# A two-layer graph network on one core: edge sums in units of two chunks, and transfers in prime numbers of rows

## The chip, the cores and the metric

The kernel runs on one core of a Trainium2 chip. The metric is device time in microseconds (us) from launch to end; lower is better. The engines are named as in the profile: PE (TensorE, matrix products), PEld (PE's loading of the stationary operand), DVE (VectorE), ACT (ScalarE), POOL (GpSimd) and SP (SyncE, which only issues transfers). Each engine executes its own instructions in the order in which they are written, and waits on semaphores for the others.

## The reference, cut to what matters

N = 6250 nodes carry 160 numbers each: 64 scalars and 32 vectors of three. E = 200000 edges run from a node `src` to a node `dst`; they are sorted by `dst`. Each edge has four attributes (`sh` in the kernel, `edge_attr_4`) and ten features (`ea`, `edge_attr_10`). There are two layers, each a sum over edges followed by small products and a normalization.

```python
# layer 0: m is bilinear in x[src] and the edge's four attributes
m_agg = segment_sum(m, dst, N)                 # (N, 160)
x = layernorm(x + (x + relu(linear(m_agg))))
# layer 1: l0, l1 = two linear maps of x times node_vec1
h = relu(edge_attr_10 @ W_fc1 / sqrt(10)) * sqrt(2)     # (E, 100)
w = h @ W_fc2 / sqrt(100)                               # (E, 192): w0 64, w1 64, w2 32, w3 32
y0, y1 = l0[src], l1[src]
m0 = w0*y0*e0;  m1 = (w1*y0) x e1;  m2 = w2*e0*y1;  m3 = w3*dot(y1, e1)
out = layernorm(x + linear(x) + linear(segment_sums of m0..m3))
```

All is float32. Because layer 0's message is linear in x[src] and in each attribute, the kernel first sums, for each destination node and each of the four attributes, attribute times x[src], and applies the weights once per node afterwards.

## The kernel before

**Chunks and windows.** The edges are padded to 391 chunks (`NCH`) of 512: 128 partitions times `J` = 4 edges. Since `dst` is sorted, the edges of one chunk end in a narrow window of at most 32 nodes (`W`; `WIDTHS` sets 16, 24 or 32 by the chunk's number, and 32 for the first three). From chunk 312 (`HALF`) on, a chunk has two windows, one for each half of the partitions. `ORDER` interleaves the chunks below `HALF` with those above; `POS` gives a chunk's place in it, and `CLOSE` the step by which a block of 128 nodes has all its edges. There are 49 blocks (`NB`). `windowed` is the path that is executed; it calls `sums(0, x)` and `sums(1, ytab)`, where `ytab` is the table of node values that layer 0 writes to DRAM.

**One chunk in layer 0.** `load` has GpSimd issue four indirect transfers (`gathered`, L206), each fetching 128 rows of x by `srcs` into one of eight buffers `g`, and now and then has SP load edge attributes (`attributes`: up to 32 chunks as four transfers of up to 32 rows into `raw`, which `turn` transposes on DVE). `onehot` builds the chunk's stationary operand on DVE: L381 compares the relative destinations with 0, 1, ... into `bank`, a PSUM tile, and L385 multiplies that by the attributes into `S`, one of three slots of `ring` (128 partitions x 4 edges x 4 attributes x 32 places, of which the first 16, 24 or 32 are written). `matmuls` adds four products on PE (L427), each S(128 x 128) transposed times g(128 x 160), into a PSUM tile `ab`; each product waits for its own gather. A chunk above `HALF` has eight products of 64 rows. `add` transposes `ab` in blocks of 32 x 32 (L447) and adds it to `acc` at the window's place (L449), both on DVE.

**One chunk in layer 1.** The sources are rows of `ytab`. `features` of four chunks are loaded by `load` as two transfers of 10 rows from `ea` (into `et` or `early`). `hidden` multiplies them by `W_fc1` for two chunks at a time (PE, `ph`, L394) and has ACT apply relu (`h`, L397). `message` works in halves of two edges per partition: two products `pw` (L407) into one of two PSUM buffers, then three DVE instructions that multiply `pw` by the gathered rows into `m` (L410, and L415 twice). `matmuls` (L427, now 320 columns) and `add` (L444, L445, L449) follow.

**Order.** `sums` writes the order by hand. In step t, each stage treats the chunk that is a fixed number of steps back, and all engines' instructions are written in this order:

```python
stages = [(load, 0), (onehot, 1), (hidden, 1), (add, 4), (message, 2), (matmuls, 3)]   # layer 1
stages = [(load, 0), (onehot, 1), (add, 3), (matmuls, 2)]                              # layer 0
```

After the stages of a step come the `parts`, which finish a block of nodes whose step has come: in layer 0 `fetch` (xt), `project` (ph, L461), `rectify` (rl, L497, and the clearing of acc, L498, on ACT), `residual` and `moments` (L471, L473), `deviation`, `normed` (L478, L480), `turned` (xp, L511, L512), `kept`, `linear` (pl, L525, L526) and `written`, which sends y to `ytab` from ACT and base to `btab` from SP; in layer 1 `fetch_base`, `project_last` (L548), `residual_last`, `deviation` and `sent`. Small weights are prepared at step 8. The four gathers of the first two chunks are issued before the window table is ready, into `early`.

So PE's order in layer 0 is: the four products of a chunk, then whatever part of a block is due. A gather may be issued when the chunk that had the same buffer eight chunks earlier has been multiplied.

## Time and profile before

The times of three runs are 4875.3, 4870.28 and 4859.52 us (median 4870.28). The profiled execution is one more.

| | |
|---|---|
| profiled execution, its own time | 4865.16 us |
| its span, first to last instruction | 4863.0 us |
| instructions | 42324 |
| mean granted clock of PE in the span | 0.752 of full speed |
| busy: PE / PEld / DVE / ACT / POOL | 2968.4 / 2222.4 / 2162.4 / 377.9 / 2973.9 us |
| gathers of x (layer 0) / of ytab (layer 1) | 1556 / 1564, 949 ns each on POOL |
| products of layer 0 (L427, g) | 3744, 716.6 us busy |
| products of layer 1 (L427, m) | 3760, 1087.9 us busy |
| pw (L407) | 3128, 737.3 us busy |
| transposes of layer 0 (L447) | 470, 361 ns each |
| messages (L410 / L415) | 782 of 420 ns / 1564 of 346 ns |
| S (L385) / one-hot (L381) | 782 of 552 ns / 782 of 256 ns |

PE shows each product as two records. How to read the views: in the table of waits a row gives the engine and line, what released it, the total, the number and the longest. In the timeline a row gives start and duration in us, engine, line, operation, output and inputs, shape, how many equal instructions follow one another, and in brackets the idle time before it and its releaser. A releaser called "remote" is a semaphore event next to which no instruction's end was recorded; "issue" is time in which the engine waited for nothing that the profile shows. The ends of PE's instructions are modelled.

### The profile page before, as it was taken

To read this page: it belongs to the slowest core of one execution; us is meant where nothing else is said; L and a number is where in the kernel's file an instruction comes from. 1 tells how busy PE (TensorE), PEld (TensorE's weight loads), DVE (VectorE), ACT (ScalarE), POOL (GpSimd) and SP (SyncE) were. 2 spreads that over 40 slices of the span, in tenths; PEclk is the share of its full clock that TensorE was granted. 3 is DMA by queue.
4 is the path that set the end of the run, shared out by engine and by line. 5 is a ranking of instruction groups with operands and counts; after the bars stand their busy time and mean duration, and the time that the engine had idled before them with its cause. 6 is when DMAs were issued, how large, how long until landed. Compare 5 with 4: busy or idle time off the path is not lost.

```text
span 4863.0 us, 42324 instructions
## 1 busy us (share of the span) xinstructions
PE 2968.4 (61%) x12714; PEld 2222.4 (46%) x12715; DVE 2162.4 (44%) x6948; ACT 377.9 (8%) x747; POOL 2973.9 (61%) x3137
## 2 busy tenths in 40 slices
PE   2333344444444444446587878777878788887777
PEld 1322333333333333434355555555555555555555
DVE  3222222232323333334355555555566566666656
ACT  2000000000000000001000000000100010101000
POOL 5666666666666666664665655565556656555553
PEclk7566655666666666667788888888888888888888
DMA  2222222222222222222222222222222222222221
GB/s 67 61 62 58 63 64 63 61 65 65 66 63 69 64 67 65 69 68 57 57 59 54 60 54 60 57 61 58 59 59 57 62 60 62 61 57 61 58 59 39
DMA packets 198246, 295.60 MB, mean 61 GB/s; under 512 B 59271, under 2 KB 140669, under 8 KB 198011
## 3 DMA queue, kind: packets, MB, share of 16 engines
q0 software_dynamic: 150144, 256.45, 21.4%
q1 hardware_dynamic: 40702, 31.55, 2.3%
q10 hardware_dynamic: 7164, 4.80, 0.3%
q8 instruction: 107, 1.75, 0.1%
q14 instruction: 129, 1.05, 0.1%
HBM read 280.57 MB, written 12.00 MB: 60 GB/s over the span
## 4 chain that ended last, share of the span: by engine, by line
PE 42%; another core or an unknown queue 33%; DVE 12%; issue 10%; POOL 2%; ACT 1%; DMA 0%; DVEq 0%; ACTq 0%; POOLq 0%
PE ab L427 24%; PE pw L407 11%; PE ph L394 3%; DVE m L415 3%; DVE S L385 2%; PE ph L461 2%; POOL g L206 2%; DVE acc L449 1%; PE bank L548 1%; DVE m L410 1%; DVE ab L444 1%; DVE ab L447 1%; DVE ab L445 1%; DVE bank L381 1%
## 5 line engine op out<-in xcount | busy, mean ns | idle before, releaser
L206 POOL DMA_INDIRECT g<-ytab,srcs x1564 | 1484.3, 949 | 1074.1 <-issue 438.5
L206 POOL DMA_INDIRECT g<-in_x,srcs x1556 | 1477.2, 949 | 741.8 <-issue 424.3
L427 PE MATMUL ab<-g,S 128*128 128x160 f32 (+1 forms) x3744 | 716.6, 392 | 818.6 <-issue 418.0
L427 PE MATMUL ab<-m,S 128*128 128x320 f32 (+1 forms) x3760 | 1087.9, 493 | 56.1 <-DVE acc L449 48.0
L427 PEld LDWEIGHTS ab<-g,S 128*128 128x128 f32 (+1 forms) x3744 | 638.5, 259 | 902.5 <-issue 441.2
L407 PE MATMUL pw<-fc,h 100*128 100x192 f32 x3128 | 737.3, 385 | 472.4 <-DVE m L415 375.1
L407 PEld LDWEIGHTS pw<-fc,h 100*128 100x128 f32 x3128 | 609.3, 222 | 703.1 <-issue 313.2
L427 PEld LDWEIGHTS ab<-m,S 128*128 128x128 f32 (+1 forms) x3760 | 698.3, 220 | 324.3 <-issue 161.9
L447 DVE STREAM_TRANSPOSE ab<-ab 128x160 f32<-128x160 f32 x470 | 169.6, 361 | 1232.0 <-remote 999.1
L385 DVE TENSOR_TENSOR S<-bank,sh 128x384 f32<-128x384 f32 (+2 forms) x782 | 431.5, 552 | 551.8 <-remote 189.8
L415 DVE TENSOR_TENSOR m<-g,pw 128x192 f32<-128x192 f32 x1564 | 475.9, 346 | 0.0
L410 DVE TENSOR_TENSOR m<-pw,g 128x256 f32<-128x256 f32 x782 | 328.1, 420 | 320.0 <-remote 208.9
L397 ACT ACTIVATE h<-ph 100x512 f32<-100x512 f32 x391 | 230.6, 597 | 2223.2 <-remote 983.1
L449 DVE TENSOR_TENSOR acc<-acc,ab 128x120 f32 (+2 forms) x940 | 261.7, 278 | 285.1 <-remote 176.3
L381 DVE TENSOR_TENSOR bank<-iota,rel 128x96 f32<-128x96 f32 (+2 forms) x782 | 200.2, 256 | 181.9 <-remote 96.9
L461 PE MATMUL ph<-wb,acc 128*128 128x160 f32 (+1 forms) x490 | 125.4, 430 | 246.9 <-DVE acc L449 107.2
L461 PEld LDWEIGHTS ph<-wb,acc 128*128 128x128 f32 (+1 forms) x490 | 109.6, 286 | 264.3 <-issue 117.1
L445 DVE STREAM_TRANSPOSE ab<-ab 32x160 f32<-32x160 f32 x470 | 165.5, 352 | 16.2
L444 DVE STREAM_TRANSPOSE ab<-ab 128x160 f32<-128x160 f32 x470 | 167.4, 356 | 10.7 <-issue 6.7
L394 PE MATMUL ph<-early,fc 10*100 10x512 f32 x392 | 114.9, 648 | 0.3
L394 PE MATMUL ph<-et,fc 10*100 10x512 f32 x390 | 112.0, 642 | 0.2 <-issue 0.2
L525 PE MATMUL pl<-wn,xT 128*128 128x320 f32 (+1 forms) x98 | 49.4, 593 | 87.1 <-issue 60.2
(80 smaller groups left out, 732.3 us busy)
## 6 DMA issues: line engine op xcount, KB each, us to landing
g<-ytab,srcs POOLq DMA_INDIRECT x1564
g<-in_x,srcs POOLq DMA_INDIRECT x1556
raw<-in_sh SPq DMA_DIRECT2D x88, 64.0 KB
early<-in_ea SPq DMA_DIRECT2D x98, 40.0 KB
xt<-in_x SPq DMA_DIRECT2D x48, 80.0 KB
ytab<-y ACTq DMA_DIRECT2D x48, 80.0 KB
btab<-base SPq DMA_DIRECT2D x48, 80.0 KB
et<-in_ea SPq DMA_DIRECT2D x96, 40.0 KB
```

The costliest lines, as they stand in the source:

```text
L206: nc.gpsimd.indirect_dma_start(out=g[:, j, :], out_offset=None, in_=table, in_offset=bass.IndirectOffsetOnAxis(ap=srcs[:, c, j:j + 1], axi ...
L381: nc.vector.tensor_tensor(oh[:, :, :w], iota[:, None, :w].to_broadcast([P, J, w]), rel[:, c, :, None].to_broadcast([P, J, w]), op=ALU.is_e ...
L385: nc.vector.tensor_tensor(S[c][:, :, :, :w], oh[:, :, None, :w].to_broadcast([P, J, 4, w]), attr[:, :, :, None].to_broadcast([P, J, 4, w]) ...
L394: nc.tensor.matmul(ph[:, i, :], fc1[g:g + 10, :], ET[c // 4][g:g + 10, c % 4 // 2, :], start=True, stop=True)
L397: nc.scalar.activation(H[c], H["p"][:, c % 2, :].rearrange("f (p j) -> f j p", j=J), AF.Relu, scale=FC_SCALE)
L407: nc.tensor.matmul(pw[:, j, :], h[:, q + j, :], fc2, start=True, stop=True)
L410: nc.vector.tensor_tensor(mq[:, :, :, 0:64], pw[:, :, 0:128].rearrange("p j (a u) -> p j a u", a=2), y[:, :, None, 0:64].to_broadcast([P, ...
L415: nc.vector.tensor_tensor(mq[:, :, a, 64:160].rearrange("p j (d u) -> p j d u", d=3), y1, pw[:, :, None, w:w + 32].to_broadcast([P, 2, 3, ...
L427: nc.tensor.matmul(ab[:, :n], one[h * i:h * i + h, j, :, :], t[h * i:h * i + h, j, :], start=(j == 0), stop=(j == J - 1), skip_group_check ...
L447: nc.vector.transpose(tr, blocks[:, 0])
L449: nc.vector.tensor_tensor(v, v, tr[:, :, :width(c)], op=ALU.add)
L461: nc.tensor.matmul(po[:r], lhs, weights[:, g, :], start=(g == 0), stop=(g == 4))
```

## The change

**Pairs.** The gather buffers become four pairs, `g` of 2 x 4 x 160, and the ring of S two pair slots. `onehot` works at every second step on two chunks: one comparison (L401), one multiplication (L408); `turn` writes the attributes in another order so that a pair's lie side by side. `WIDTHS` puts the first four chunks at width 32 where it were three. In layer 1 `onehot` stands one step later.

**Layer 0's sums.** For two chunks below `HALF`, `matmuls` issues one product of eight columns (one from each of the pair's gather buffers) into a spare part of the PSUM tile (L461), and then the eight products (L467). A chunk above `HALF` is a unit by itself, with four columns. In the built program all the waits for gathers then stand ahead of L461, and the products after it carry none. `add` transposes the pair with one instruction (L480); the additions stay one per window (L496). There are two PSUM tiles of two banks where there were four of one.

**Layer 1's messages.** The four `pw` products of a chunk (L430) go to one tile of two banks, of which there is one, and three DVE instructions (L433, and L438 twice) make the chunk's messages.

**Transfers.** The features are first copied, in eight parts during layer 0, from `ea` to a DRAM table `etab` of 17 rows (ten, and seven of them again), and layer 1 loads 17 rows from it, three steps earlier than before and ahead of the gathers' step (`features`). Edge attributes are loaded as groups of 30 chunks in transfers of 31 rows (or 17, 19, 23 or 29), one transfer per step over four steps, and `raw` is always cleared first. Blocks of 128 rows (xt, base, ytab, btab, out) are sent as 94 and 34 rows.

**In the built programs** SP's issues rise from 530 to 738 and ACT's from 49 to 95; GpSimd's gathers stay as they are. PE's stand-alone waits go from 476 to 1010 in layer 0 and from 944 to 551 in layer 1; PE's instructions that post to its semaphore go from 1687 to 439 and from 1881 to 1562. DVE's element-wise instructions go from 1256 to 864 and from 3594 to 2033.

```diff
-WIDTHS = ((3, 32), (128, 16), (208, 24), (HALF, 32), (NCH, 24))
+WIDTHS = ((4, 32), (128, 16), (208, 24), (HALF, 32), (NCH, 24))
...
+LEADS = 94
+ROWS = 17
+STEP = 30
+COPIES = 8
+LEAD = 3
...
+def group(c):
+    begin, end = (0, HALF) if c < HALF else (HALF, NCH)
+    first = c - (c - begin) % STEP
+    return first, 31 if end - first >= STEP else next(n for n in (17, 19, 23, 29, 31) if n >= end - first)
...
-    ring = const.tile([P, 3, J, 4, W], F32, name="S")
+    ring = const.tile([P, 2, 2, J, 4, W], F32, name="S")
...
-            pa = s.enter_context(tc.tile_pool(name=f"pa{layer}", bufs=3 if layer else 4, space=PSUM))
+            pa = s.enter_context(tc.tile_pool(name=f"pa{layer}", bufs=3 if layer else 2, space=PSUM))
...
-                pp = s.enter_context(tc.tile_pool(name="pp", bufs=2, space=PSUM))
+                pp = s.enter_context(tc.tile_pool(name="pp", bufs=1, space=PSUM))
...
             def load(c):
+                i, half = divmod(POS[c], 2)
+                if not half:
+                    GP[i] = early if not layer and c in ahead else gp.tile([P, 2, J, D], F32, name="g")
+                G[c] = GP[i][:, half]
                 if layer or c not in ahead:
+                    gathered(nc, G[c], srcs, table, c)
+                for first, n in GROUPS:
+                    for q in range(4):
+                        if POS[c] == fetched[first] + (q if POS[first] >= fetched[first] + 4 else 0):
+                            attributes(first, n, q)
...
             def onehot(c):
+                if POS[c] % 2:
+                    return
+                n = min(2, NCH - c)
...
+                oh = bank[:, :n * J * W].rearrange("p (j n) -> p j n", n=W)
+                nc.vector.tensor_tensor(oh[:, :, :w], iota[:, None, :w].to_broadcast([P, n * J, w]),
+                                        rel[:, c:c + n, :].rearrange("p c j -> p (c j)")[:, :, None].to_broadcast([P, n * J, w]),
+                                        op=ALU.is_equal)
+                pair = ring[:, POS[c] // 2 % 2]
...
             def message(c):
...
-                for q in range(0, J, 2):
-                    pw = pp.tile([P, 2, 192], F32, name="pw")
...
+                pw = pp.tile([P, J, 256], F32, name="pw")
+                for j in range(J):
+                    nc.tensor.matmul(pw[:, j, 0:192], h[:, j, :], fc2, start=True, stop=True)
...
+            def unit(c):
+                if layer or c >= HALF:
+                    return [c]
+                return [c - 1, c] if POS[c] % 2 else []

             def matmuls(c):
...
+                    both = PA["unit", c] = pa.tile([P, 2, 512], F32, name="ab")
+                    PA[c] = [both[:, i, :n + D] for i in range(2)]
+                    rows = GP[POS[c] // 2][:, :, :, 0:1] if len(chunks) > 1 else G[c][:, None, :, 0:1]
+                    nc.tensor.matmul(both[:, 0, n + D:n + D + J * len(chunks)], S[chunks[0]][:, 0, :, :],
+                                     rows.rearrange("p a j o -> p (a j o)"), start=True, stop=True, skip_group_check=True)
...
             def add(c):
...
+                    nc.vector.transpose(both[:, :, D:2 * D], both[:, :, 0:D])
...
+            def sent_rows(engine, b, to, from_):
+                cut = LEADS if CLOSE[b] < NCH - 8 and rows(b) == P else rows(b)
+                for part in (slice(0, cut), slice(cut, rows(b))):
+                    if part.start < part.stop:
+                        engine.dma_start(to[part], from_[part])
...
-                stages = [(load, 0), (onehot, 1), (hidden, 1), (add, 4), (message, 2), (matmuls, 3)]
+                stages = [(load, 0), (features, -LEAD), (onehot, 2), (hidden, 1), (add, 4), (message, 2), (matmuls, 3)]
...
+                if not layer and t >= 2 * PREPARE and t % 32 == 0 and t // 32 <= COPIES:
+                    part = slice((t // 32 - 1) * (NCH * CH // COPIES), t // 32 * (NCH * CH // COPIES))
+                    nc.sync.dma_start(etab[0:10, part], ea[:, part])
+                    nc.sync.dma_start(etab[10:ROWS, part], ea[0:ROWS - 10, part])
```

## The prediction

> **What bounds the kernel now.** I read the table by stage first, because the page's shares average two unlike layers. I set its four stretches by GpSimd's gathers: first free gather to last of layer 0, the gap between the layers, the gathers of layer 1, the end. The columns are the stretch, its length, and the busy time and instructions of PE, PEld, DVE, ACT and POOL, then the granted clock and the DMA share.
>
> ```profile
> 31.80:2248.40 2216.60, 916.03 (x4378) 775.84 (x4378) 645.25 (x1995) 123.08 (x273) 1476.28 (x1556) 0.63 0.26 65
> 2248.40:2291.80 43.40, 33.24 (x180) 22.15 (x180) 22.60 (x77) 10.97 (x33) 0.96 (x2) 0.80 0.11 32
> 2291.80:4806.80 2515.00, 1973.11 (x7899) 1392.37 (x7900) 1436.16 (x4649) 238.32 (x428) 1483.37 (x1563) 0.85 0.23 59
> 4806.80:4863.00 56.20, 45.97 (x258) 32.06 (x258) 42.96 (x145) 5.54 (x12) 0.95 (x1) 0.99 0.07 18
> ```
>
> No engine is full in either layer. GpSimd comes nearest: each gather is 949 ns busy and is followed by 0.30 us that the waits call issue, so 1.2525 us at best (timeline: 1211.19, 1212.44, 1213.69, 1214.95). A chunk has four, 5.01 us. Layer 0's 1556 steps need 1949 us of 2217, so GpSimd stood still for 268; layer 1's 1564 need 1958 of 2515, so 557. The whole span is then 32 + 1949 + 268 + 43 + 1958 + 557 + 56 = 4863. Without the stalls, 4038 is the floor that this change leaves, as it removes no gather. So the question is who makes GpSimd wait. The first two rows below are waits of layer 0 (100 to 2250 us), the rest of layer 1 (2292 to 4807): engine, line, releaser, total us, times, longest.
>
> ```profile
> DVE ab L447 <- remote: 964.9, 131, 22.4
> ACT rl L497 <- remote: 714.1, 18, 361.7
> ...
> POOL g L206 <- DVE bank L381: 383.6, 103, 8.8
> PE pw L407 <- DVE m L415: 375.1, 100, 29.1
> ...
> DVE m L410 <- remote: 208.9, 76, 11.9
> DVE S L385 <- remote: 189.8, 29, 20.6
> POOL g L206 <- DVE m L415: 172.5, 49, 7.0
> ```
>
> "Remote" is a release near which no instruction ends. With one core there is no other core, and L447 waits for PE alone. The timeline shows what it is (PE's rows, then DVE's, then GpSimd's):
>
> ```profile
> 1184.81 3.63 PE L427 MATMUL ab<-g,S 128*128 128x160 f32 x24
> 1196.40 3.00 PE L461 MATMUL ph<-wb,acc 128*128 128x160 f32 x10 [7.96 <-DVE ab L447]
> 1199.19 3.86 PE L427 MATMUL ab<-g,S 128*128 128x160 f32 x16
> 1217.44 0.47 PE L511 MATMUL xp<-ident,z 128*128 128x128 f32 x1 [14.39 <-DVE rs L478]
> ...
> 1210.96 0.37 DVE L447 STREAM_TRANSPOSE ab<-ab 128x160 f32<-128x160 f32 x1 [13.87 <-remote]
> ...
> 1216.63 0.28 DVE L449 TENSOR_TENSOR acc<-acc,ab 128x120 f32 x1 [5.31 <-remote]
> ...
> 1211.19 0.95 POOL L206 DMA_INDIRECT g<-in_x,srcs  x1 [2.78 <-remote]
> ```
>
> By the program's counts, the transpose at 1210.96 waits for the last of the three chunks in the run of 24, which ended at 1188.4. Its completion was seen 22 us late, and GpSimd's gather, which needs the same buffer back, was freed by it too. PE meanwhile waited for DVE (14.39). So the bound is a ring in which PE, DVE and GpSimd wait for completions of PE that are posted late. PE's semaphore shows how: in such stretches its updates come singly, at 1199.73, 1203.93, 1208.13, 1210.93 and 1216.61; later nine come 0.04 us apart (1218.02 to 1218.36). One update is one instruction that posts, whatever its step.
>
> I counted those instructions in the built programs: 1687 in layer 0 and 1881 in layer 1 before; 2217 / 1687 = 1.31 us and 2515 / 1881 = 1.34 us for each. The likeness suggests that posting is the pace of both layers; it does not prove it.
>
> **The change, part by part.**
>
> *Layer 0's sums by pairs.* Before, every product of a chunk waits for its own gather and posts by itself: eight posts for two chunks. After, all waits stand before one small product, and the eight follow without a wait and post once. Posts fall from 1687 to 439. Here the page "TensorE: Matmul & The Clock Gate", section "The cost: per-tile semaphore tail", speaks against a gain: it prices a serial completion increment at about 26 ns. By that, 1248 fewer posts are 33 us of latency, nearly all under GpSimd's 5.01 us a chunk, and the change gives layer 0 nothing. The bursts (40 ns) fit the rule; the 1.4 to 5.7 us between single posts do not. I take the row: at 1.31 us, 439 posts need 575 us in 1949, and the layer goes at GpSimd's pace. The worst spacing above, 5.7 us, for 439 posts is 2500 us, but that worst case was not met on average even by the old layer. I leave 30 us of stall (bounds 5 and 150), which is 238 us off.
>
> *What it adds there.* 235 waiting products, 8 columns wide; no row shows one. Nearest is xp at 0.35 us, two records each: 235 x 0.7 = 165 us of PE, which is busy 916 of 2217 us; hidden. Without the cover, those 165. A pair's products now start when its eighth gather has landed, 5 us later than the first chunk's did; four pairs of buffers (40 us of gathers) cover that. PE's stand-alone waits rise from 476 to 1010; behind them queue only products that need the same gathers.
>
> *One-hots and S by pairs.* From L381 (96 columns 257 ns, 128 columns 290) and L385 (384: 558, 512: 692) a column costs 1.03 and 1.05 ns. A pair at width 24 is 0.36 + 0.96 = 1.32 us against 2 x 0.815: 0.16 us less per chunk. Layer 0's transposes (160: 361 ns) become one of 320, 0.53 by that slope: 0.10 less. In layer 0 both are hidden by the gathers. What counts in layer 1 is the distance: S has two pair slots, whose last readers ran two steps before, where the old third slot was read in the step just before. The wait of L385 (remote 190, PE ab 150, PE ph 74, over 1.0 us per chunk) goes. It returns in part at the transposes of the sums, which now wait for the same product of the step before.
>
> *Messages in three instructions.* 2 x (420 + 2 x 346) = 2.22 us per chunk become, at 1.16 ns a column (346 to 420 for 64 columns), 0.72 + 2 x 0.57 = 1.86: 0.37 less, 145 us of DVE in the layer. Posts of pw: two to one. Against it: pw has a single buffer, so the next four products wait for all three messages. Their cover on PE is the sums of the chunk before: about 2.1 us at full clock, more otherwise, and half a ph.
>
> *Layer 1's sum.* PE is busy 1973 / 391 = 5.05 us per chunk, and that work stays. Its wait for messages was 375 / 391 = 0.96. Posts fall from 1881 to 1562, so the pace of 1.34 would give 2093 us, 5.35 per chunk. From below GpSimd gives 5.01; from above 6.43 (no gain). I take PE's 5.05 plus 0.4 for what remains of its waits: 5.45, near the count of posts. Stalls: (5.45 - 5.01) x 391 = 172 instead of 557, 385 us off.
>
> *Transfers in odd numbers of rows.* The page "DMA: Bandwidth & Descriptors", section "Why a DMA increments its semaphore by 16 and not by 1", says that the engines used are the largest number up to 16 that divides the slowest dimension: 17 or 31 rows go to one, 94 and 34 to two. That speaks against this part. Queue q1's 40702 packets took 2.3% of 16 engines, 44 ns for 775 B; by size 2 KB is an estimated 116 ns. A feature load (17 rows, 34 packets) is then 3.9 us on one engine. Four chunks have two: 7.9 us in 20, and by the rule a quarter of that engine is gathers'. Full it is not, and loads are issued three steps earlier. I take 0 (bounds -30 to +60; a share of the late posts could be DMA completions' fault). The issues on SP rise from 530 to 738; over 4.8 ms that is one in 6.5 us.
>
> *Copies of the features, eight of 1.7 MB, and DVE's clearing of raw (under 0.5 us, 26 times).* By the same packet rate, a copy is some 4 us on ten engines; a gather may land late, which the eight in flight (10 us) absorb. I take 10 us, bounds 0 and 60.
>
> Sum: 4863 - 238 - 385 + 10 = 4250. The profiled execution took 4865.16 us for its span of 4863.0, and the median of the runs is 4870.28; I add nothing more, 4250.
>
> **The rivals.**
>
> *Only layer 0 gains.* Layer 1's loop of messages keeps 6.43 us because the single pw buffer takes the place of the S wait. For it: PE waits more for messages than anything else. Against it: PE runs the sums just then. 4038 + 30 + 557 + 10 = 4635.
>
> *Late posts are not a matter of their number.* If what delays a post is PE's waiting itself, fewer posts wait longer each, and more stand-alone waits make it no better. Layer 0 keeps its stalls, DVE's shorter work is hidden: 4863 less at most some 100 us of messages, 4760 to 4870.
>
> *The single buffer makes it slower.* At half clock (layer 1 has 0.85 on average) four pw products take 2.6 us, twice the 1.28 of full clock; a late post like those of L410 (208.9 / 76 = 2.75 us) and 1.86 us of messages make 7.2 in series if PE's sums cover nothing. Layer 1 is then 391 x 7.2 = 2815, the total 4038 - 1958 + 2815 + 30 + 10 = 4935. It decides from 7.05 us per chunk on, if layer 0 gains, as that eats 238 + 557.
>
> **How the numbers follow.** Both layers gain: 0.72, by itself 4090 to 4440 (layer 1 at 5.05 to 5.9 us). Only layer 0: 0.16. Not a matter of number: 0.06, a quarter of it within 0.3%. Slower: 0.06. The range must reach to the rival at 4635 to leave out no more than 2 in 10: 4080 to 4640. 0.3% of 4870, 15 us, is about what the measurement can tell from no change. Faster 0.92, same 0.02, slower 0.06.
>
> **What would show it.** Layer 0's gathers at 1.25 us without gaps, in 1.96 to 2.0 ms; L447's successor without remote waits of 10 us and more; DVE's S without a wait on PE in layer 1; gathers there in 2.0 to 2.3 ms; messages at 0.72 and 0.57 us. The prediction is wrong if the remote waits stay as long with a quarter of the posts, if PE's wait for messages grows beyond 1 us per chunk, or if gathers wait for their own landing behind one loaded DMA engine.

## The result

The changed kernel is slower: 5009.94 us median (4986.77 to 5021.54) beside 4872.78 us (4859.52 to 4875.3) for the kernel before, a ratio of 1.0281 with a 95% interval of 1.024 to 1.0323. The forecast was 4250 us, in a range of 4080 to 4640. Its profiled execution took 4986.77 us, with a span of 4985.0 us.

The table by stage of the changed kernel, with edges at its own first and last gathers (stretch, length, busy time and instructions of PE, PEld, DVE, ACT and POOL, granted clock, DMA share, GB/s):

```profile
32.40:2256.60 2224.20, 994.42 (x4848) 847.70 (x4850) 576.87 (x1400) 122.38 (x275) 1474.52 (x1555) 0.65 0.27 71
2256.60:2300.10 43.50, 34.06 (x184) 22.73 (x180) 19.45 (x59) 9.86 (x31) 0.95 (x1) 0.77 0.12 32
2300.10:4936.50 2636.40, 1935.41 (x7938) 1361.37 (x7940) 1354.37 (x3148) 240.65 (x431) 1484.48 (x1564) 0.83 0.23 58
4936.50:4985.00 48.50, 38.91 (x220) 26.89 (x217) 34.54 (x98) 4.05 (x9) 0.91 (x1) 0.96 0.07 19
```

Layer 0 takes 2224 us where it took 2217, although its PE now posts 439 times and not 1687. Layer 1 takes 2636 where it took 2515; that is 121 of the 122 us that the spans differ by. DVE's work in layer 1 fell from 1436 to 1354 us and bought nothing.

The groups of the page that answer to the edits (busy time and mean ns, then idle time before and its main releaser):

```profile
L480 DVE STREAM_TRANSPOSE ab<-ab 128x320 f32<-128x320 f32 x235 | 123.9, 527 | 1417.1 <-remote 1148.6
L433 DVE TENSOR_TENSOR m<-pw,g 128x512 f32<-128x512 f32 x391 | 270.1, 691 | 801.5 <-remote 390.7
L461 PE MATMUL ab<-g,S 128*128 128x8 f32 (+1 forms) x468 | 105.8, 298 | 560.0 <-issue 382.8
L438 DVE TENSOR_TENSOR m<-g,pw 128x384 f32<-128x384 f32 x782 | 394.1, 545 | 0.0
L408 DVE TENSOR_TENSOR S<-bank,sh 128x768 f32<-128x768 f32 (+2 forms) x392 | 370.1, 944 | 13.4
```

The instructions cost what was estimated, and S's idle time went from 551.8 to 13.4 us. But the remote wait of layer 0's transpose, 964.9 us in 131 places before, is 1144.2 us in 99. ("Remote" stands here for completions of PE that are seen late, as the prediction read it.) The table of waits, the first two rows from 100 to 2250 us and the others from 2400 to 4900:

```profile
DVE ab L480 <- remote: 1144.2, 99, 27.4
...
POOL g L219 <- remote: 239.9, 73, 5.7
...
PE pw L430 <- DVE m L438: 441.8, 103, 11.8
...
POOL g L219 <- DVE m L438: 392.9, 72, 12.6
...
DVE m L433 <- remote: 369.7, 60, 8.8
POOL g L219 <- DVE bank L401: 276.7, 52, 9.5
...
DVE m L433 <- DMA g<-ytab,srcs: 119.3, 47, 5.5
```

The last row is new beside the kernel before: messages wait for gathers that have not landed. GpSimd is held for up to 12.6 us, and then PE and DVE overtake it.

The timeline of layer 0 shows a late completion from both sides:

```profile
1335.77 3.25 PE L467 MATMUL ab<-g,S 128*128 128x160 f32 x10
...
1340.69 0.30 PE L467 MATMUL ab<-g,S 128*128 128x160 f32 x1 [1.68 <-issue]
...
1343.36 0.94 POOL L219 DMA_INDIRECT g<-in_x,srcs  x1 [0.30 <-issue]
1343.48 0.42 PE L467 MATMUL ab<-g,S 128*128 128x160 f32 x1 [2.49 <-issue]
1344.88 0.43 PE L467 MATMUL ab<-g,S 128*128 128x160 f32 x1 [0.98 <-issue]
1346.28 0.63 PE L467 MATMUL ab<-g,S 128*128 128x160 f32 x1 [0.97 <-issue]
1347.68 0.42 PE L467 MATMUL ab<-g,S 128*128 128x160 f32 x1 [0.77 <-issue]
1348.38 0.42 PE L467 MATMUL ab<-g,S 128*128 128x160 f32 x1 [0.28 <-issue]
1348.48 0.53 DVE L480 STREAM_TRANSPOSE ab<-ab 128x320 f32<-128x320 f32 x1 [13.62 <-remote]
1348.72 0.95 POOL L219 DMA_INDIRECT g<-in_x,srcs  x1 [4.41 <-remote]
```

These products wait for nothing that the profile shows, and still their starts fall 0.7, 1.4 or 2.8 us apart. The last of them starts 4 us after GpSimd has run out of buffers (its last gather ended at 1344.3); DVE's transpose and GpSimd's next gather follow at once.

### The profile page after: what moved, and what is told of

The parts are those of the page before. It is cut to its first block, busy times and chain, and to the rows that moved or that the text cites. A ratio compares the mean times of both kernels' runs of the same rounds, so it can differ in the third digit from the quotient of the medians.

```text
span 4985.0 us, 40848 instructions
## 1 busy us (share of the span) xinstructions
PE 3002.8 (60%) x13184; PEld 2258.7 (45%) x13185; DVE 2001.0 (40%) x4786; ACT 376.9 (8%) x747; POOL 2973.2 (60%) x3137
## 4 chain that ended last, share of the span: by engine, by line
PE 35%; another core or an unknown queue 23%; issue 15%; POOL 14%; DVE 9%; DMA 3%; DVEq 0%; ACT 0%; POOLq 0%; ACTq 0%
PE ab L467 19%; POOL g L219 14%; PE pw L430 11%; DVE m L438 3%; PE ph L418 3%; DMA g<-ytab,srcs 2%; DVE m L433 2%; DVE S L408 1%; PE ph L515 1%; DMA g<-in_x,srcs 1%; DVE acc L496 1%; PE ab L461 1%; PE bank L602 1%; DVE bank L401 1%
## 5 line engine op out<-in xcount | busy, mean ns | idle before, releaser
L467 PE MATMUL ab<-m,S 128*128 128x320 f32 (+1 forms) x3760 | 1069.4, 491 | 57.9 <-issue 29.4
L430 PE MATMUL pw<-fc,h 100*128 100x192 f32 x3128 | 709.8, 378 | 642.7 <-DVE m L438 475.7
L430 PEld LDWEIGHTS pw<-fc,h 100*128 100x128 f32 x3128 | 593.0, 218 | 869.2 <-issue 768.8
L467 PE MATMUL ab<-g,S 128*128 128x160 f32 (+1 forms) x3744 | 743.1, 396 | 275.3 <-issue 264.3
L467 PEld LDWEIGHTS ab<-m,S 128*128 128x128 f32 (+1 forms) x3760 | 682.6, 219 | 323.9 <-issue 172.0
L467 PEld LDWEIGHTS ab<-g,S 128*128 128x128 f32 (+1 forms) x3744 | 638.9, 261 | 299.3 <-issue 297.5
L480 DVE STREAM_TRANSPOSE ab<-ab 128x320 f32<-128x320 f32 x235 | 123.9, 527 | 1417.1 <-remote 1148.6
L433 DVE TENSOR_TENSOR m<-pw,g 128x512 f32<-128x512 f32 x391 | 270.1, 691 | 801.5 <-remote 390.7
L461 PE MATMUL ab<-g,S 128*128 128x8 f32 (+1 forms) x468 | 105.8, 298 | 560.0 <-issue 382.8
L438 DVE TENSOR_TENSOR m<-g,pw 128x384 f32<-128x384 f32 x782 | 394.1, 545 | 0.0
L461 PEld LDWEIGHTS ab<-g,S 128*128 128x128 f32 x468 | 102.8, 267 | 628.1 <-issue 538.9
L408 DVE TENSOR_TENSOR S<-bank,sh 128x768 f32<-128x768 f32 (+2 forms) x392 | 370.1, 944 | 13.4
L496 DVE TENSOR_TENSOR acc<-acc,ab 128x120 f32 (+2 forms) x940 | 261.8, 278 | 185.6 <-remote 107.5
L493 DVE STREAM_TRANSPOSE ab<-ab 128x160 f32<-128x160 f32 x470 | 168.9, 359 | 329.2 <-remote 124.1
L401 DVE TENSOR_TENSOR bank<-iota,rel 128x192 f32<-128x192 f32 (+2 forms) x392 | 138.9, 354 | 99.1 <-remote 68.8
```

What stands on the lines that cost most here:

```text
L401: nc.vector.tensor_tensor(oh[:, :, :w], iota[:, None, :w].to_broadcast([P, n * J, w]), rel[:, c:c + n, :].rearrange("p c j -> p (c j)")[:, ...
L408: nc.vector.tensor_tensor(pair.rearrange("p c j k n -> p (c j) k n")[:, :n * J, :, :w], oh[:, :, None, :w].to_broadcast([P, n * J, 4, w]), ...
L430: nc.tensor.matmul(pw[:, j, 0:192], h[:, j, :], fc2, start=True, stop=True)
L433: nc.vector.tensor_tensor(mq[:, :, :, 0:64], pw[:, :, 0:128].rearrange("p j (a u) -> p j a u", a=2), y[:, :, None, 0:64].to_broadcast([P, ...
L438: nc.vector.tensor_tensor(mq[:, :, a, 64:160].rearrange("p j (d u) -> p j d u", d=3), y1, pw[:, :, None, w:w + 32].to_broadcast([P, J, 3, ...
L461: nc.tensor.matmul(both[:, 0, n + D:n + D + J * len(chunks)], S[chunks[0]][:, 0, :, :], rows.rearrange("p a j o -> p (a j o)"), start=True ...
```

## The experiments

Edits are told against the kernel that is named. Kernels of one group ran on one chip, with the kernel before among them, and ratios are taken within a group. The first comparison, of before and after, is a group of its own. One thing has to be known: in groups 2 and 3 the kernel before took 3980 and 3982 us, in the others 4928, 4877 and 4875; group 2 and group 5 used the same chip. In groups 2 and 3 no completion was late, and with the edits of the kernel before GpSimd issued without a gap. The kernel with seven buffers in layer 1 shows it; its layer 0 is that of before. Its layer 0 in group 3 (from 32 to 2000 us), and the wait of its transposes from 100 to 1950 us, where the kernel before had waited for "remote":

```profile
32.00:2000.00 1968.00, 1442.31 (x4558) 918.89 (x4558) 680.76 (x2072) 134.25 (x306) 1473.58 (x1556) 0.57 0.27 73
...
DVE ab L447 <- PE ab L427: 1000.6, 357, 4.6
```

The longest wait is 4.6 us and not 22.4, and no wait of that table is put down to "remote". Layer times in the table are from first to last gather of the profiled execution.

| group | kernel | time, us | ratio to before (95%) | layer 0 | layer 1 |
|---|---|---|---|---|---|
| 1 | messages of before | 4994.27 | 1.0146 (1.0101 to 1.0191) | 2234 | 2623 |
| 1 | transfers of before | 5054.77 | 1.0249 (1.0186 to 1.0313) | 2232 | 2707 |
| 1 | one-hots by chunk in layer 1 | 5090.95 | 1.0352 (1.0303 to 1.0402) | 2233 | 2719 |
| 1 | single-chunk gather buffers in layer 1 | 4870.15 | 0.9892 (0.9846 to 0.9938) | 2237 | 2500 |
| 2 | before, seven buffers in layer 1 | 3981.44 | 1.0004 (0.9995 to 1.0012) | 1945 | 1955 |
| 2 | single buffers and messages of before | 4008.31 | 1.0068 (1.0051 to 1.0084) | 1962 | 1963 |
| 2 | more products in layer 0 | 4009.62 | 1.0073 (1.0053 to 1.0093) | 1962 | 1959 |
| 2 | narrow gathers in layer 0 | 3991.63 | 1.0033 (1.0021 to 1.0045) | 1947 | 1957 |
| 3 | the changed kernel again | 4012.17 | 1.0073 (1.0056 to 1.0089) | 1962 | 1959 |
| 3 | before, pairs of buffers in layer 1 | 3983.15 | 1.0001 (0.9993 to 1.001) | 1946 | 1956 |
| 3 | before, seven buffers in layer 1 | 3983.46 | 1.0002 (0.9994 to 1.0011) | 1946 | 1956 |
| 3 | more products in layer 0 | 4010.56 | 1.007 (1.005 to 1.009) | 1964 | 1960 |
| 4 | before, pairs of buffers in layer 1 | 5007.12 | 1.0278 (1.0221 to 1.0335) | 2218 | 2644 |
| 4 | transfers of before | 4972.97 | 1.0187 (1.0142 to 1.0233) | 2219 | 2636 |
| 4 | more products in layer 0 | 4892.58 | one run | 2265 | 2485 |
| 5 | before, seven buffers in layer 1 | 4872.26 | 0.9999 (0.9979 to 1.0019) | 2216 | 2511 |
| 5 | single buffers and transfers of before | 4821.52 | 0.9893 (0.987 to 0.9915) | 2217 | 2483 |
| 5 | narrow gathers in layer 0 | 4832.74 | one run | 2220 | 2479 |

### Four parts of the change, each undone

After the first comparison the theories were: A, the single pw buffer puts late completions and messages in series; B, the pairs of gather buffers shorten GpSimd's lead; C, the transfers load few DMA engines.

Messages of before, in the changed kernel:

```diff
-pp = s.enter_context(tc.tile_pool(name="pp", bufs=1, space=PSUM))
+pp = s.enter_context(tc.tile_pool(name="pp", bufs=2, space=PSUM))
...
-                pw = pp.tile([P, J, 256], F32, name="pw")
+                for q in range(0, J, 2):
+                    pw = pp.tile([P, 2, 192], F32, name="pw")
...
```

> The changed kernel with the messages of before (two halves, six instructions, two pw buffers). Theory A, the single pw buffer puts PE's late completions and the messages in series: layer 1 falls from 2636 us to about 2520 (as before), the total to about 4890. Theory B, pairs of gather buffers: layer 1 stays within 30 us of 2636, since only 145 us of hidden DVE work come back. Theory C, transfers on few DMA engines: stays too. Layer 0 stays at 2224 in all.

Transfers of before, in the changed kernel:

```diff
-STEP = 30
+STEP = 32
...
-    return first, 31 if end - first >= STEP else next(n for n in (17, 19, 23, 29, 31) if n >= end - first)
+    return first, min(STEP, end - first)
...
-                cut = LEADS if CLOSE[b] < NCH - 8 and rows(b) == P else rows(b)
+                cut = rows(b)
...
-                        nc.sync.dma_start(et[64 * i:64 * i + ROWS, :, :], etab[...])
+                        nc.sync.dma_start(et[64 * i:64 * i + 10, :, :], ea[...])
...
-                    nc.sync.dma_start(etab[0:10, part], ea[:, part])
-                    nc.sync.dma_start(etab[10:ROWS, part], ea[0:ROWS - 10, part])
```

> The changed kernel with the transfers of before (no etab, 10, 32 and 128 rows, one transfer each; features still three steps early). Theory C, rows in prime numbers load one or two DMA engines and gathers land late: DVE's 119 us of waits for landed gathers in layer 1 go and the total falls by 60 to 120 us. Theories A and B: within 20 us of the changed kernel.

One-hots by chunk in layer 1:

```diff
-                if POS[c] % 2:
+                if POS[c] % 2 and not layer:
                     return
-                n = min(2, NCH - c)
+                n = 1 if layer else min(2, NCH - c)
...
-                pair = ring[:, POS[c] // 2 % 2]
+                pair = ring[:, POS[c] // 2 % 2, POS[c] % 2:]
```

> The changed kernel with layer 1's one-hots and S built for each chunk by itself (four slots, lag two as in the changed kernel). DVE has 0.16 us more a chunk. If the pair's longer instructions (1.3 us at once) hold up messages, layer 1 falls by 20 to 60 us; by theories A, B and C it moves by less than 20 us.

Gather buffers of one chunk in layer 1:

```diff
                 i, half = divmod(POS[c], 2)
-                if not half:
+                if layer:
+                    G[c] = gp.tile([P, J, D], F32, name="g1")
+                elif not half:
...
+        with tc.tile_pool(name="gl", bufs=GRING) as gp:
+            sums(1, ytab, gp, hp)
```

> The changed kernel with layer 1's gather buffers of one chunk each (eight, as before) in place of four pairs. Theory B, a pair's first gather waits for the messages of the pair's second chunk, so the depth is seven chunks and not eight: layer 1's stalls of 680 us fall by about 100 and the total to about 4900. Theories A and C: within 20 us.

Only the buffers bring back more than the loss: ratio 0.9892, with layer 1 at 2500 us. Theory B is right about the place. With the transfers undone the kernel is still 2.5% slower than before (1.9% in group 4), so C is not the cause of the loss in layer 1. With the messages of before the interval (1.0101 to 1.0191) ends below that of the changed kernel in its own comparison (from 1.024), so beside the pairs the new messages cost about 1.3%. The edit undoes the single pw buffer and the longer instructions together; as the longer ones are less work for DVE, the buffer is the likelier part, but that was not separated. It is not what decides, since the kernel with single gather buffers has these messages too and is faster than before. One-hots by chunk were to gain 20 to 60 us in layer 1 or to change little; they gave 1.0352 and 2719 us there. The intervals overlap, so that a loss is not certain; why there should be one is open.

What the buffers changed in layer 1, from the table of waits from 2400 to 4700 us, the changed kernel first:

```profile
POOL g L219 <- DVE m L438: 327.1, 61, 12.6
POOL g L219 <- DVE bank L401: 273.2, 51, 9.5
DVE m L433 <- DMA g<-ytab,srcs: 100.8, 41, 5.5
```

```profile
POOL g L219 <- DVE m L441: 191.8, 63, 6.6
POOL g L219 <- DVE bank L404: 162.7, 65, 5.1
...
DVE m L436 <- DMA g<-ytab,srcs: 8.3, 9, 1.8
```

GpSimd's longest stops are half as long, and messages hardly ever find gathers missing.

### Pairs of buffers alone, and seven buffers, in the kernel before

Is it the depth that the pairs take away, or the pair itself? Two edits of the kernel before, in layer 1 alone:

```diff
-                if layer or c not in ahead:
-                    G[c] = gathered(nc, gp.tile([P, J, D], F32, name="g"), srcs, table, c)
+                if layer:
+                    i, half = divmod(POS[c], 2)
+                    if not half:
+                        G["pair"] = gp.tile([P, 2, J, D], F32, name="g")
+                    G[c] = gathered(nc, G["pair"][:, half], srcs, table, c)
...
+        with tc.tile_pool(name="gl", bufs=GRING // 2) as gp:
+            sums(1, ytab, gp, hp)
```

```diff
+        with tc.tile_pool(name="gl", bufs=7) as gp:
+            sums(1, ytab, gp, hp)
```

Seven buffers, group 2; then pairs and seven buffers, group 3:

> The kernel before with seven gather buffers in layer 1 in place of eight, nothing else. Theory B, the depth of the gather buffers is what the pairs took away: layer 1 grows by 60 to 190 us, and the total is 1 to 4% above before. If depth is not what counts (only that a pair's eight gathers are released at once), it stays within 0.5% of before.

> The kernel before with one part of the change alone: layer 1's gather buffers are four pairs. Where completions are late, the pairs alone give layer 1 at least the 120 us that the whole change lost there: ratio 1.02 to 1.04. If the pairs cost only together with the single pw buffer, within 0.5% of before. Where gathers run without gaps: within 0.3%.

> The kernel before with seven gather buffers in layer 1. Where completions are late: layer 1 grows by 60 to 190 us if depth is what counts, and by less than 20 us if it is the release of eight gathers at once. Where gathers run without gaps: within 0.3%, as it was there.

In groups 2 and 3 nothing stalls, and both are within 0.1% of before. So the pairs by themselves cost nothing there. Once more where completions are late, the pairs in group 4 and seven buffers in group 5:

> The kernel before with four pairs of gather buffers in layer 1, nothing else. Where completions are late: layer 1 grows by at least 120 us, ratio 1.02 to 1.04, if the pairs by themselves are the cause; within 0.5% of before if they cost only together with the single pw buffer or the longer one-hots. Where completions are in time: within 0.3%, as it was.

> The kernel before with seven gather buffers in layer 1. Where completions are late: if depth counts, layer 1 grows by 60 to 130 us (ratio 1.012 to 1.027); if it is the release of eight gathers at once, by less than 20 us (within 0.4%). Where they are in time: within 0.3%, as it was twice.

The pairs alone give 1.0278, as much as the whole change (1.0281). Seven buffers give 0.9999: depth is not the cause, and theory B's reason falls while its place stands. Each stands beside the kernel before of its own group (4877 and 4875 us). The two programs differ in one thing. A pair's first gather waits for exactly the value of DVE's semaphore that the same gather waits for with seven buffers (all 187 such waits beyond the first 64 gathers are equal); with seven buffers GpSimd waits 192 more times, at the second chunk of each pair. PE's and DVE's posts are the same in number (3567 and 4844). So **192 waits were taken from GpSimd, none was added, and the kernel became 2.8% slower**.

GpSimd's timeline, the last gather of a run and the next, from 3000 to 3060 us; with seven buffers:

```profile
3013.50 0.95 POOL L206 DMA_INDIRECT g<-ytab,srcs  x1 [0.30 <-issue]
3017.60 0.95 POOL L206 DMA_INDIRECT g<-ytab,srcs  x1 [3.16 <-DVE bank L381]
...
3021.62 0.95 POOL L206 DMA_INDIRECT g<-ytab,srcs  x1 [0.30 <-issue]
3024.88 0.94 POOL L206 DMA_INDIRECT g<-ytab,srcs  x1 [2.31 <-DVE bank L381]
...
3038.65 0.94 POOL L206 DMA_INDIRECT g<-ytab,srcs  x1 [0.30 <-issue]
3044.01 0.95 POOL L206 DMA_INDIRECT g<-ytab,srcs  x1 [4.41 <-DVE bank L381]
```

and with pairs:

```profile
3013.80 0.95 POOL L206 DMA_INDIRECT g<-ytab,srcs  x1 [0.30 <-issue]
3023.20 0.94 POOL L206 DMA_INDIRECT g<-ytab,srcs  x1 [8.45 <-DVE bank L386]
...
3031.93 0.95 POOL L206 DMA_INDIRECT g<-ytab,srcs  x1 [0.30 <-issue]
3037.43 0.94 POOL L206 DMA_INDIRECT g<-ytab,srcs  x1 [4.55 <-DVE bank L386]
```

I counted such runs of gathers and the stop behind each (over 0.4 us longer than the pace), from the traces, in layer 1 from 2400 us on. The commonest lengths are:

| kernel, layer | gathers in the run: number of runs, median stop in us |
|---|---|
| seven buffers, layer 1 | 4: 47, 1.4; 8: 42, 2.4; 12: 80, 4.0 |
| pairs, layer 1 | 8: 72, 2.5; 16: 56, 7.5 |
| before, layer 0 | 4: 16, 2.1; 12: 10, 2.2; 16: 12, 2.8; 20: 23, 3.4; 24: 15, 4.0; 32: 4, 4.8 |
| changed, layer 0 | 8: 15, 1.9; 16: 27, 2.8; 24: 25, 4.1; 32: 5, 5.3 |

The longer GpSimd issues without a stop, the longer its next stop. That alone proves little: in layer 0, from 12 gathers on, a stop is 0.15 to 0.19 us for each gather of the run, and with seven buffers 0.30 to 0.36, as it would be behind any consumer of even pace. What stands out is the pair's run of 16. With seven buffers a run that passes 8 nearly always ends at 12 and costs 4.0 us, 0.33 a gather. A pair cannot stop at 12: it goes on to 16 and costs 7.5, 0.47 a gather. The commonest stops sum to 47 x 1.4 + 42 x 2.4 + 80 x 4.0 = 487 us and 72 x 2.5 + 56 x 7.5 = 600 us; layer 1 differs by 2644 - 2511 = 133.

The traces also show where the longer stop comes from. DVE's first instruction behind a run starts 2.2 us after the last gather's end, behind 12 with seven buffers as behind 16 with pairs (medians); only the next gather differs, 4.3 and 7.9 us after it. With pairs, PE begins 4.1 to 4.5 products (its records) per us in the first 10 us of a run of gathers, 1.1 between 12 and 15 us, and 0.4 between 15 and 20 us. So it is the last four gathers of a run of 16, 5 us, in which PE hardly moves; what it has not done by then, it does while GpSimd stands still.

### What holds PE's completions up

Eight more products behind each unit of layer 0, and, in another kernel, gathers of 128 bytes a row there (each product reads the 32 columns five times, so layer 0's sums are not the reference's). Both have single-chunk gather buffers in layer 1.

```diff
+                if not layer:
+                    for k in range(8):
+                        nc.tensor.matmul(both[:, 1, n + D:n + D + P], ident, ident, start=True, stop=True, skip_group_check=True)
```

```diff
-        nc.gpsimd.indirect_dma_start(out=g[:, j, :], out_offset=None, in_=table,
+        nc.gpsimd.indirect_dma_start(out=g[:, j, :n], out_offset=None, in_=table.rearrange("n (a d) -> (n a) d", d=n),
```

Where completions turned out to be in time (groups 2 and 3):

> The changed kernel with single-chunk gather buffers in layer 1, and in layer 0 eight more products of a constant (128 x 128 by 128) behind each unit's, that wait for nothing and whose results nobody reads. If PE's completions are late because PE is left without work behind them, or by its low clock, layer 0's stalls of about 290 us fall below 100 us. If they are late whatever PE does next, the stalls stay at 290 us or grow, as PE's time grows by 1 to 2 us a pair.

> The changed kernel with single-chunk gather buffers in layer 1, and in layer 0 gathers of 128 bytes a row in place of 640 (each product reads the 32 columns five times, so layer 0's sums are not the reference's). GpSimd issues as many gathers at the same pace, with as many descriptors. If the gathers' bytes hold up PE's completions, layer 0's stalls of about 290 us fall below 100 us. If it is GpSimd's issuing or the number of descriptors, or PE alone, they stay within 60 us of 290.

> Single-chunk gather buffers in layer 1, and eight more products of a constant behind each unit of layer 0. Where completions are late: layer 0's stalls of about 290 us fall below 100 us if PE's completions are late because PE has no work behind them or a low clock; they stay or grow if they are late whatever PE does. Where gathers run without gaps: about 18 us of stalls, as it was there.

Where they were late (groups 4 and 5, one run each):

> Single-chunk gather buffers in layer 1, and eight more products of a constant behind each unit of layer 0. Where completions are late: layer 0's stalls of about 290 us fall below 100 us if PE's completions are late for want of work behind them or by a low clock; they stay or grow if they are late whatever PE does. Where completions are in time: 18 us of stalls.

> Single-chunk gather buffers in layer 1, and in layer 0 gathers of 128 bytes a row in place of 640 (layer 0's sums are not the reference's). Where completions are late: layer 0's stalls of about 290 us fall below 100 us if the gathers' bytes hold up PE's completions; they stay within 60 us of it if it is the issuing, the descriptors or PE alone. Where they are in time: about 6 us of stalls, as it was.

Where completions are late, layer 0 stands still for 321 us with more products and for 278 with narrow gathers, beside 278 in the changed kernel (the sum of GpSimd's gaps over its own pace). With more products, from 100 to 2250 us:

```profile
DVE ab L486 <- remote: 972.9, 113, 17.3
...
POOL g L219 <- remote: 230.2, 88, 3.5
```

- *Work behind a product* doesn't bring its completion. (In the built program the gather buffers are released by a post that stands ahead of the extra products; the transposes wait for the last of them.)
- *PE's clock* isn't it. Layer 0's granted clock was 0.75 with more products and 0.63 in the kernel before, late in both, and 0.57 in the row of group 3 above, where nothing was late.
- *The bytes of the gathers* don't delay it, and the gathers themselves are not late: from the start of a gather on GpSimd to the end of its last packet in layer 0 it is 2.25 us in the kernel before and 2.20 with seven buffers in group 3 (medians).
- *The loading of instructions* (queues q8 and q14) has a packet in the 10 us ahead of a stop or in the stop in 18 of the 89 stops of layer 0 before, so most stops have none.
- *The number of posts* doesn't count either: the kernel before posts 1687 times in layer 0 and stands still for 268 us.

Apart from the kernel with more products, all traces of late groups have layer 0 between 2216 and 2237 us, 1.42 to 1.44 us a gather.

That GpSimd's own run of issues holds the completions up fits all of this: PE's pace that falls as a run goes on, DVE's work that comes back some 2 us after the run's end in layer 1, the harm of waits taken away. It was not tried by stopping GpSimd on purpose, and each of its gathers had 128 rows in every run, so it is inferred, not shown. Why there is none of it in groups 2 and 3, where GpSimd issues without a stop, stays open; the same chip showed both. The times listed for these groups come with a span and a clock each, that is, from traced executions, so whether the tracing takes part can't be told either.

### What the change costs where nothing stalls

The changed kernel again (group 3), the transfers of before (group 4), and single gather buffers with the messages of before (group 2) or with the transfers of before (group 5):

> The changed kernel once more, beside the others. Where PE's completions come late (the chip of the first comparison, and that of the four undoings) its ratio to before is about 1.028; where GpSimd's gathers run without gaps (the chip of the second four, before at 3980 us) there is no stall to lose or to gain, and it is 1.005 to 1.010 (layer 0's start and the longer way of the last chunks).

> The changed kernel with the transfers of before. Where completions are in time: the 16 us that layer 0 lost (stalls near the eight copies of the features) go, ratio 1.002 to 1.005 in place of 1.0073. Where they are late: 1.02 to 1.03 as before, since the gain drowns in layer 1's stalls.

> The changed kernel with layer 1's gather buffers of one chunk each and the messages of before (halves, six instructions, two pw buffers). If the single pw buffer costs by itself what it cost beside the pairs of buffers (about 1.4% of the time), the ratio falls from 0.989 to about 0.975. If late completions only showed because the depth was short, it stays within 0.5% of 0.989.

> The changed kernel with layer 1's gather buffers of one chunk each and the transfers of before: what is left is layer 0's units, the one-hots by pairs and the messages in three instructions. Where completions are late: 0.985 to 0.992, as with the pairs undone alone. Where they are in time: 1.002 to 1.004, since the stalls by the copies go and the longer gap between the layers stays.

In group 3 the changed kernel is 30 us slower, 1.0073. Layer 0 has 16 of them. GpSimd's gaps of over 0.6 us in its steady part lie at 173, 333, 451, 593, 796, 972, 1133 and 1307 us, each 10 to 18 us behind one of SP's eight pairs of issues for the copies of the features (at 155, 315, 440, 582, 785, 961, 1123 and 1297); by these gaps alone about 13 us. With narrow gathers layer 0 took 1947 us, copies and all, which fits a competition of the two for transfer; the copies were not taken out where completions are in time. The gap between the layers grew from 24 to 35 us. GpSimd's longest wait there, first with seven buffers (group 3), which leave layer 0 as it was, then in the changed kernel:

```profile
POOL g L206 <- DMA btab<-base: 22.9, 1, 22.9
```

```profile
POOL g L219 <- DMA ytab<-y: 34.1, 1, 34.1
```

These 11 us are not the transfers' alone: the four kernels of groups 2 and 3 that have the same transfers, but single-chunk gather buffers in layer 1, have 26 to 29 us there (one profiled execution each). Where completions are late, the changed kernels with the transfers of before have this gap at 40, 32 and 34 us, and the changed kernel and the one with single buffers at 44, as the kernel before (43) has with its own transfers. With them undone the ratio in group 4 (1.0187) is below the changed kernel's interval and in group 1 (1.0249) within it, so that part of the change costs between nothing and 0.9% there.

The kernel with single buffers and the transfers of before has 0.9893 (0.987 to 0.9915), the same as with the transfers of the change (0.9892 in group 1), and beats both kernels where completions are late. It was not run where they are in time; its kin with the new transfers lose 0.7% there. Whether the single pw buffer costs anything beside single gather buffers where completions are late is open too, since that kernel ran only in group 2 (1.0068; the whole change had 1.0073 in group 3).

## Why the prediction was wrong

**What bounds the kernel: half right.** GpSimd's gathers were called the floor, 4038 us with the gaps of start and end as they were. Groups 2 and 3 show it reached: there the layers of before run at 1.251 us a gather, and the whole takes 3980 us. That GpSimd stands still for late completions of PE was right.

**"Posting is the pace of both layers": the first step that failed.** It rested on two quotients that came out alike, 1.31 and 1.34 us for each post. Posts fell from 1687 to 439 and layer 0's stop went from 268 to 278 us, where 30 were forecast. So the 238 us of gain did not come. The rule of the Trainium skill that was set aside there ("TensorE: Matmul & The Clock Gate", "The cost: per-tile semaphore tail": about 26 ns an increment, by which layer 0 gains nothing) gave the right sum, though it says nothing of completions that come 20 us late. The rival "late posts are not a matter of their number", given 6%, describes layer 0 as measured. The three signs of being wrong that the prediction named all came: the remote waits stayed as long, PE's wait for messages went beyond 1 us a chunk, and messages waited for gathers to land (119 us).

**Layer 1's sum, 5.45 us a chunk: the second.** Measured: 2636 / 391 = 6.74, that is 505 us over the 2131 forecast. PE's own work was right (1935 / 391 = 4.95, forecast 5.05); the 0.4 for "what remains of its waits" was 1.8. Two things were in it. With single gather buffers the layer still takes 2500 us, 6.4 a chunk: some 370 us of the 505 are the late completions, which fewer posts did not take away here either. The other 136 came with the pairs of gather buffers, which the step left out; it had met them in layer 0 only ("four pairs of buffers cover that"). By themselves they cost 2.8%. They could not have been costed as depth: by that count they are never worse than seven buffers, which cost nothing. The trace of before showed layer 1's stops of 4.0 us behind runs of 12 gathers (87 from 2400 us on), and the program that pairs would go on to 16. That they lengthen the run could have been counted; what a run of 16 costs could not be read from that trace.

The two steps, 248 us in layer 0 and 505 in layer 1, are more than the whole distance from 4250 to the measured span of 4985; the copies and the end gave back the rest.

**The single buffer of pw: right in kind.** It was part of the 0.4 us a chunk, and at 4935 us a rival of 6%. Beside the pairs the new messages cost about 1.3%, some 0.17 us a chunk; PE's wait for messages went from 375 to 476 us in the layer (0.96 to 1.22 us a chunk). That the kernel came out slower, as this rival said, is luck: layer 0 gained nothing, and the pairs alone cost as much as the whole change.

**Sizes that held.** The messages took 691 and 545 ns (forecast 720 and 570), the transpose of 320 columns 527 (530), one-hot and S of a pair of width 24 in the timeline 0.36 + 0.96 = 1.32 us (1.32), the waiting products 106 us of PE (165). S's wait on PE went, and came back in part at the transposes of the sums, as said (L493 is idle 329 us before it starts). All of it lay beside GpSimd's stops.

**Transfers.** They were taken as 0 with bounds of -30 and +60, and the copies as 10 us. In group 3 the copies' gaps are about 13 us, and 11 more are lost between the layers, which the sum had not; what of these the transfers cost is open. The way to the 10 us was wrong: at the rate used, 2 KB in 116 ns, 1.7 MB on ten engines are 9.6 us and not 4, and in the trace of group 3 a copy's packets span 10 to 19 us. That it came near is luck. The few engines show: of the two feature loads of four chunks at most 2 packets are under way at once, and the two loads take 6.6 us in the median; in the kernel before it was up to 13 packets and 0.9 us. By the ratios with the transfers undone, all of this cost little.

## What to carry to other kernels

A wait is not only a cost. GpSimd, which runs ahead of everyone, was slowed by a wait at every chunk. With half of these waits gone it ran longer and stopped longer, and the kernel lost 2.8% where PE's completions were late, and nothing (1.0001) where they were in time. So when a change makes buffers coarser, count how the engine that fills them will run and stop, and not only how deep the ring is. And two quotients that agree in one trace are no mechanism: the number of posts had to be changed by itself to see whether the stops follow it.

## What was not expected of the hardware

The same kernel took 3980 us in some groups and 4870 to 4930 in others, on one chip in both ways, each within 1% inside its group; the difference lies in GpSimd's stops for PE's late completions, since within a run the gathers issue at 1.25 us in both. Where completions are late, products that wait for nothing start at multiples of 0.70 us: in layer 0 of the changed kernel, of the gaps between products of L467, 38 are 0.70, 78 are 1.40, 46 are 2.10 and 17 are 2.80 us, to within 0.03. In group 3 the same kernel has none of these. And in layer 1 with pairs PE begins 4 products and more per us while a run of gathers is young, and 0.4 once GpSimd has issued for 15 us.
